# A first linear map in seven block products, and running sums kept in PSUM

## The chip, the cores and the metric

The kernel runs on one core of a Trainium2 chip. A core has a matrix engine (TensorE, PE in the profile), a vector engine (VectorE, DVE), a scalar engine (ScalarE, ACT), a general engine (GpSimd, POOL) and SyncE (SP), which here only issues transfers (DMA). Each works through its own instructions in order and waits on semaphores for the others. SBUF is the working memory of 128 partitions; PSUM, eight banks of 512 floats per partition, is where TensorE puts its results and can add to what is there. The metric is the device time of one execution in microseconds (us): the median of the timed runs.

## The reference

Two layers on x of shape (B, N, C) = (16, 1024, 256), all in float32. Each layer computes h = relu(layernorm(x)) and adds its result to x.

```
# layer 0, per batch: a graph product, then attention with 4 heads
Wg   = adj * A_s(channel means of h)
g    = relu(einsum('bcn,bnm->bcm', h^T, Wg) * para);  q from g
k, v = h @ kv_w
x    = x + softmax(q k^T * scale) v
# layer 1
A_hat = (A + I) * dinv[:, None] * dinv[None, :]
agg   = einsum('nm,bmd->bnd', A_hat, h)
z     = relu(batchnorm(agg @ W1.T + b1))      # 512 features
out   = batchnorm(z @ W2.T + b2)              # 256 features
x     = x + out
```

The batch normalizations take mean and variance over all 16 x 1024 rows. So everything up to the first map (agg @ W1.T + b1) is done for all batches, and only then does the second map start.

## The kernel before

**Stages.** The first stage runs over the 16 batches. For batch b its order on TensorE is: attention of b (`attention`, L351: four steps of eight score tiles and eight value products), the graph product of b+1 with its k, q and v (`graph`, L291), and then the two parts of layer 1 for batch b: the A_hat stage and the first map (`linear1`, L533, and `linear1_out`, L616). The second stage reads the results of the first map (z1) back from memory, normalizes them and does the second map, in pairs of column blocks. At the end (L1128 to L1170) the output is scaled by the second batch normalization, turned by TensorE, added to x1 (the output of layer 0, read back from memory) and stored.

**Order.** Nothing is reordered by a scheduler: each engine's instructions stand in the order in which the code issues them. Work of other batches is placed by hand. `graph` has a list `between` of steps to run ahead of its block c (L796 to L815), `linear1` has three hooks (`between[0]` to `between[2]`, L591 to L614). `more(c)` makes f_w, the weighted adjacency of block c of the next batch (two passes on ScalarE, one on VectorE, L262 to L266); `turn_h` transposes h of the next batch, 32 x 32 blocks on VectorE (L278) and 32 small DMAs issued by POOL (L285). `prepare_start` and `prepare_end` normalize the input of batch b+2 (statistics on VectorE, the inverse root on POOL, eight passes on ScalarE); `prepare_row` sends the channel sums to memory and back as a row (L248, L249); `again` loads x once more.

**A_hat stage.** agg is a product of 2 x 2 blocks done with seven block products instead of eight. The sums and differences of h are made on VectorE (L544 to L547); those of A_hat (`thirds`) are made once and loaded per batch. Each product fills a PSUM bank of its own with four matmul calls, and VectorE adds the banks up (L593 to L613).

**First map.** For each half g of the columns (512 nodes) and each of the four blocks of 128 features, two calls over the two halves of the 256 channels: 16 calls per batch. ScalarE adds the bias while it copies to SBUF (L637), for the last two blocks of a batch VectorE (L635). VectorE then takes batch statistics (L641), and SP stores z (L642). Batch 15 has an order of its own (`very_last`). Batch 14's first-layer work comes after the attention of batch 15, directly ahead of that of batch 15; its third hook (L845) holds the last part of batch 15's attention, its normalization and the turning of W2.

**Buffers.** `ps_s` has three PSUM buffers of two banks (score tiles, products, map results); a new tile takes the buffer that was given up first. `pp` has eight SBUF buffers of 4 KB per partition (score exponentials, `thirds`, turned h) and two more for accumulators; `w4` has five (f_w, para, agg, z).

**End.** `AHEAD` (L25) is the number of batches of x1 that are loaded ahead (`load_x1`, L871, 1 MB each, in buffers of 8 KB that the second stage also uses). z2, the output of the second map, holds the nodes in their order; x1 is loaded with eight consecutive nodes per partition. So `scaled` (L1134) reads z2 in steps of eight elements into a second tile, and TensorE turns that one:

```
src = src.rearrange("p (q i) -> p i q", i=NC)[:, i0:i1, :]
```

Of the kernel before, what the change touches and what calls it, by code (L numbers as in the profile page):

```python
# [17 lines left out]
P = 128  # L18
# [5 lines left out]
I32 = mybir.dt.int32  # L24
AHEAD = 7  # L25
LIMIT = 1e18
# [3 lines left out]
def fast_path(  # L30
# [34 lines left out]
    x1_d = [dram.tile([N, C], F32, tag=f"fx1_{b}", name=f"fx1_{b}") for b in range(B)]  # L65
    row_d = [dram.tile([N], F32, tag=f"frow_{b}", name=f"frow_{b}") for b in range(B)]
    t_d = [dram.tile([P, 4, 512], F32, tag=f"ft_{k}", name=f"ft_{k}") for k in range(3)]
    z1_d = [dram.tile([P, FC, 512], F32, tag=f"fz1_{t}", name=f"fz1_{t}") for t in range(TT)]
# [86 lines left out]
    with ExitStack() as stage:  # L155
# [377 lines left out]
        def linear1(b, h1, thirds, between):  # L533
# [14 lines left out]

            def product(ps, left, right):
                for m in range(KH):  # L550
                    nc.tensor.matmul(  # L551
                        ps,
                        left[:, m, :],
                        right(m),
                        start=(m == 0),
                        stop=(m == KH - 1),
                    )

# [27 lines left out]
            ]  # L586
            m1 = new(1)
            product(m1, a(0, 0), resident(0, 0))
            u1 = kept(1)
            nc.scalar.copy(u1, m1)  # L590
            m2 = new(2)  # L591
            product(m2, a(0, 1), resident(1, 0))
            nc.vector.tensor_add(agg[0][:, 0, :], u1, m2)  # L593
            m6 = new(6)
            product(m6, s2, third(0))
            u2 = kept(2)
            nc.vector.tensor_add(u2, u1, m6)
            between[0]()
            m7 = new(7)
            product(m7, s3, third(1))  # L600
            u3 = kept(3)
            nc.vector.tensor_add(u3, u2, m7)
            between[1]()
            m5 = new(5)
            product(m5, s1, resident(0, 1))
            nc.vector.tensor_add(agg[1][:, 1, :], u3, m5)
            nc.vector.tensor_add(u2, u2, m5)
            m4 = new(4)
            product(m4, a(1, 1), third(2))
            nc.vector.tensor_sub(agg[0][:, 1, :], u3, m4)  # L610
            m3 = new(3)
            product(m3, s4, resident(1, 1))
            nc.vector.tensor_add(agg[1][:, 0, :], u2, m3)  # L613
            between[2](agg)  # L614

        def linear1_out(b, g, aggT, parts=range(0, FC, 2)):  # L616
            t = NH * b + g
            for f2 in parts:
                ps = ps_s.tile([P, 2, 512], F32, tag="s", name=f"f_zps_{t}_{f2}")
                z = w4.tile([P, 2, 512], F32, tag="w4", name=f"f_z1_{t}_{f2}")  # L620
                for i in range(2):
                    f = f2 + i
                    for d in range(CC):
                        nc.tensor.matmul(  # L624
                            ps[:, i, :],
                            w1T[:, d, ts(f, P)],
                            aggT[:, d, :],
                            start=(d == 0),
                            stop=(d == CC - 1),
                        )  # L630
                for i in range(2):
                    f = f2 + i
                    if g + 1 == NH and f2 + 2 == FC and b + 1 < B:

                        nc.vector.tensor_scalar_add(z[:, i, :], ps[:, i, :], b1_t[:, f : f + 1])  # L635
                    else:
                        nc.scalar.activation(  # L637
                            z[:, i, :], ps[:, i, :], AF.Identity, bias=b1_t[:, f : f + 1]
                        )
                for i in range(2):  # L640
                    nc.vector.bn_stats(st1[:, f2 + i, t, :], z[:, i, :])  # L641
                nc.sync.dma_start(z1_d[t][:, f2 : f2 + 2, :], z)  # L642

        def linear1_all(b, h1, thirds, early, late, last):


            def second(agg):
                linear1_out(b, 0, agg[0])
                last()
                linear1_out(b, 1, agg[1])  # L650

            def very_last(agg):

# [12 lines left out]

            linear1(b, h1, thirds, [early, late, second if b + 1 < B else very_last])

# [10 lines left out]


        ahatT = big.tile([P, NC, N], F32, tag="ahatT", name="f_ahatT")
        deg = small.tile([P, NC], F32, tag="deg", name="f_deg", bufs=1)
        rsum = small.tile([P, NC], F32, tag="rsum", name="f_rsum", bufs=1)
# [4 lines left out]
        def turn_adj(i, copy):  # L688
            ps = ps_s.tile([P, NC, P], F32, tag="s", name=f"f_adjps_{i}")
            for m in range(NC):  # L690
                nc.tensor.transpose(ps[:, m, :], adj_t[i][:, ts(m, P)], ident)
            copy(ahatT[:, :, ts(i, P)], ps)

# [13 lines left out]
        def diagonal():  # L707
            on = unused("d").rearrange("p (m q) -> p m q", q=P)
            for m in range(NC):
                block = ahatT[:, m, ts(m, P)]  # L710
                nc.gpsimd.tensor_mul(on[:, m, :], block, ident)
                nc.gpsimd.tensor_add(block, block, ident)
            nc.vector.tensor_reduce(diag, on, AX.X, ALU.add)
# [6 lines left out]
        def roots_row():  # L720
            t = pp.tile([P, N], F32, tag="p", name="f_drow")
            ps = ps_s.tile([P, NC, P], F32, tag="s", name="f_drowps")
            for c in range(NC):
                nc.tensor.transpose(ps[:, c, :], dinv[:, c : c + 1].to_broadcast([P, P]), ident)
            nc.scalar.copy(t, ps.rearrange("p c q -> p (c q)"))
            drow.append(t)
# [14 lines left out]
        with tc.manual_schedule(engines={ENG.PE, ENG.Activation, ENG.DVE, ENG.Pool, ENG.SP}):  # L741
# [17 lines left out]
            def turn_w1():  # L759
# [9 lines left out]
                    4: [lambda: weights(0, 6), lambda: prepare_end(1), lambda: again(0)],  # L769
                    5: [lambda: weights(0, 7)],  # L770
                    7: [lambda m=m: row_sums(m) for m in range(4)],
# [5 lines left out]
            for b in range(B):  # L777
# [14 lines left out]
                def more(c):  # L792
# [4 lines left out]
                    0: [  # L797
                        more(2), lambda: turn_h(b + 1), left[0], left[1], left[2], more(3),
                        left[3], left[4], more(4),
# [65 lines left out]
    with ExitStack() as stage:  # L865
        big = stage.enter_context(tc.tile_pool(name="fbig2", bufs=1))
        io = stage.enter_context(tc.tile_pool(name="fio", bufs=AHEAD))

        xts = {}

        def load_x1(b):  # L871

            xts[b] = io.tile([P, NC, C], F32, tag="x1", name=f"f_x1t_{b}")
            nc.sync.dma_start(xts[b], x1_d[b].rearrange("(p i) d -> p i d", i=NC))

        st2 = big.tile([P, CC, TT, 6], F32, tag="st2", name="f_st2")
        with tc.manual_schedule(engines={ENG.PE, ENG.Activation, ENG.DVE, ENG.Pool, ENG.SP}):
# [39 lines left out]
            class Pair:  # L917
# [5 lines left out]
                def load(self):  # L923
                    p = self.p
                    t0, t1 = self.t

                    def two(name):
                        t = io.tile([P, 2, 2, 512], F32, tag="x1", name=f"f_z{name}_{p}")
                        return t[:, 0], t[:, 1]

                    self.t2, self.t3 = two("t23")
                    one, other = two("b1")
                    self.b[0, 0] = fetch(t0, 0, one)
                    self.b[1, 0] = fetch(t0, 2)
                    self.b[0, 1] = fetch(t1, 0, other)
                    one, self.t4 = two("b2")
                    self.b[1, 1] = fetch(t1, 2, one)

# [86 lines left out]
            def fetch_all(t):  # L1025
                z = io.tile([P, FC, 512], F32, tag="x1", name=f"f_zz_{t}")
                nc.sync.dma_start(z, z1_d[t])
                for f2 in range(0, FC, 2):
                    zs[t, f2] = z[:, f2 : f2 + 2, :]

# [24 lines left out]
            for p in SEVEN:  # L1055
# [20 lines left out]
                else:  # L1076
                    for t in rest:
                        fetch_all(t)
                    for t in range(TT - 2, TT):
                        for f2 in range(0, FC, 2):  # L1080
                            zs[t, f2] = fetch(t, f2)
                    for n in range(AHEAD):
                        load_x1(n)
# [40 lines left out]


            turned_z = {}

            def finish(b, c, i0, i1):  # L1128
                if i0 == 0:
                    turned_z[b, c] = lasting.tile(  # L1130
                        [P, NC, P], F32, tag="z", name=f"f_zo_{b}_{c}", bufs=4
                    )

                def scaled(out, src):  # L1134
                    src = src.rearrange("p (q i) -> p i q", i=NC)[:, i0:i1, :]
                    s, t = bn2.s[:, c : c + 1], bn2.t[:, c : c + 1]
                    if c == 0:
# [4 lines left out]
                if b + 1 < B:  # L1142
                    scaled(turned_z[b, c][:, i0:i1, :], z2[:, c, b, :])
                else:
                    for g in range(NH):
                        scaled(turned_z[b, c][:, i0:i1, ts(g, P // NH)], last[g, c])

            for b in range(B):
# [3 lines left out]
                for i0 in range(0, NC, 4):  # L1152
                    ps = ps_out.tile([P, 4, C], F32, tag="out", name=f"f_outps_{b}_{i0}")
                    for c in range(CC):
                        if b == 0:
                            finish(b, c, i0, i0 + 4)
                        for i in range(4):
                            nc.tensor.transpose(
                                ps[:, i, ts(c, P)], turned_z[b, c][:, i0 + i, :], ident
                            )  # L1160
# [4 lines left out]
                for i0, ps in zip(range(0, NC, 4), outs):  # L1165
                    here = xt[:, i0 : i0 + 4, :]
                    nc.vector.tensor_add(here, here, ps)
# [517 lines left out]
```

## Time and profile before

| what | us |
|---|---|
| median of three runs | 2504.25 (2500.96 to 2507.36) |
| the profiled execution | 2502.86 |
| its span | 2501.1 |
| mean granted clock of TensorE | 0.992 of full speed |

The span runs from the first to the last instruction of the profiled execution; the 1.8 us around it are the launch. The costliest groups on TensorE, by line (a matmul call of float32 is recorded as two instructions; "busy" counts overlapped instructions once):

| line | what | records | busy, us |
|---|---|---|---|
| L362 | attention scores | 2048 | 458.1 |
| L403 | attention values | 2048 | 453.6 |
| L308 | graph product | 1024 | 444.7 |
| L551 | A_hat stage (four groups) | 896 | 398.0 |
| L326, L341 | k, q and v | 768 | 227.7 |
| L624 | first map | 512 | 222.5 |

A row of the profile's groups gives line, engine and operation, then output and inputs with their shapes, the number of instructions, their busy time and mean duration in ns, and last the idle time of the engine just before them with what ended it. A row of a timeline gives start, length, engine, line, operation and, in brackets, the idle time before it and its releaser. The chain of waits follows the work that ended last back through its releasers.

### The profile page before, as it was taken

How to read it: one execution, taken by the hardware profiler on the slowest of the kernel's cores; microseconds unless marked ns; L12 is line 12 of the kernel's file. 1: busy time of each engine (PE TensorE's matmuls, PEld its weight loads, DVE VectorE, ACT ScalarE, POOL GpSimd, SP SyncE). 2: the span in 40 equal slices, each digit the busy share in tenths (PEclk: the TensorE clock that was granted, in tenths of full speed). 3: DMA queues.
4: the chain of work that ended last, by engine and by line, in shares of the span. 5: the costliest groups of instructions: out<-in, count | busy, mean ns of one | idle time of the engine just before them, and what ended most of it. 6: DMA issues, size and time to landing. Idle time of an engine off the chain costs nothing.

```text
span 2501.1 us, 24402 instructions
## 1 busy us (share of the span) xinstructions
PE 2432.2 (97%) x8122; PEld 1074.5 (43%) x8122; DVE 1625.7 (65%) x2223; ACT 1302.0 (52%) x1854; POOL 328.1 (13%) x577
## 2 busy tenths in 40 slices
PE   7999999999999999999999999999999999999984
PEld 4443444434343434344443434343444434444443
DVE  4786667484838475665848393857667586567665
ACT  7845545454636464554536363645555456256543
POOL 2030202020110302020202002030202020000012
PEclk9999999999999999999999999999999999999997
DMA  5031414131322324141322232242424120445549
GB/s 168 7 129 59 135 59 135 59 104 53 107 84 63 115 62 132 59 135 59 118 70 87 71 94 91 59 127 59 135 60 135 59 68 29 148 172 180 212 159 355
DMA packets 169239, 263.42 MB, mean 105 GB/s; under 512 B 37009, under 2 KB 120465, under 8 KB 166545
## 3 DMA queue, kind: packets, MB, share of 16 engines
q1 hardware_dynamic: 148944, 229.23, 28.4%
q0 software_dynamic: 20160, 32.55, 4.1%
q8 instruction: 66, 1.08, 0.2%
q14 instruction: 69, 0.56, 0.1%
HBM read 157.82 MB, written 70.31 MB: 91 GB/s over the span
## 4 chain that ended last, share of the span: by engine, by line
PE 82%; DMA 7%; DVE 5%; ACT 3%; issue 1%; SPq 1%; POOL 1%; DVEq 0%; POOLq 0%; ACTq 0%
PE f_s L362 15%; PE f_o L403 15%; PE f_aps L551 15%; PE f_gps L308 13%; PE f_zps L624 8%; PE f_vps L341 4%; PE f_kps L326 4%; PE f_zx L953 3%; PE f_zm L953 2%; DMA out_dram<-f_x1t 2%; PE f_z2ps L889 2%; DVE f_acc L379 1%; DMA f_hT<-f_hQ 1%; SPq L467 1%; DMA frow<-f_sums 1%
## 5 line engine op out<-in xcount | busy, mean ns | idle before, releaser
L370 ACT ACTIVATE f_p<-f_s 128x1024 f32<-128x1024 f32 x512 | 477.3, 1046 | 145.4 <-PE f_s L362 144.0
L379 DVE TENSOR_TENSOR f_acc<-f_acc,f_p 128x1024 f32<-128x1024 f32 x384 | 470.5, 1225 | 41.1 <-DVE f_acc L379 1.4
L362 PE MATMUL f_s<-f_qT,f_kT 64*128 64x512 f32 x2048 | 458.1, 596 | 0.0
L403 PE MATMUL f_o<-f_p,f_v 128*64 128x512 f32 x2048 | 453.6, 595 | 0.0
L308 PE MATMUL f_gps<-f_w,f_h_a 128*128 128x512 f32 x1024 | 444.7, 594 | 2.2 <-DVE f_w L266 2.2
L285 POOL DMA_DIRECT2D f_hT<-f_hQ x480 | 235.7, 499 | 1226.0 <-DVE f_hQ L278 838.3
L362 PEld LDWEIGHTS f_s<-f_qT,f_kT 64*128 64x128 f32 x2048 | 189.4, 185 | 265.9 <-ACT f_p L370 121.6
L308 PEld LDWEIGHTS f_gps<-f_w,f_h_a 128*128 128x128 f32 x1024 | 192.8, 190 | 250.4 <-issue 229.3
L403 PEld LDWEIGHTS f_o<-f_p,f_v 128*64 128x64 f32 x2048 | 141.4, 137 | 304.3 <-issue 274.0
L624 PE MATMUL f_zps<-f_aggT,f_w1T 128*128 128x512 f32 x512 | 222.5, 592 | 0.0
L266 DVE SCALAR_TENSOR_TENSOR f_w<-f_w,f_adj 128x1024 f32<-128x1024 f32 x128 | 155.1, 1213 | 83.2 <-ACT f_w L265 76.2
L262 ACT ACTIVATE f_w<-f_row,f_col 128x1024 f32<-128x1024 f32 x128 | 148.2, 1158 | 52.3 <-DMA f_row<-frow 47.7
L637 ACT ACTIVATE f_z<-f_zps,f_b 128x512 f32<-128x512 f32 x98 | 62.1, 684 | 202.9 <-PE f_zps L624 202.9
L219 ACT ACTIVATE f_h_a<-f_x,f_shift_a,f_rstd_a 128x256 f32<-128x256 f32 x128 | 75.0, 587 | 175.5 <-DVE f_shift_a L214 175.5
L641 DVE BATCH_NORM_STATS2 f_st<-f_z 128x6 f32<-128x512 f32 x128 | 82.2, 684 | 124.6 <-ACT f_z L637 124.6
L219 ACT ACTIVATE f_h_b<-f_x,f_shift_b,f_rstd_b 128x256 f32<-128x256 f32 x128 | 64.6, 587 | 170.7 <-DVE f_shift_b L214 170.7
L624 PEld LDWEIGHTS f_zps<-f_aggT,f_w1T 128*128 128x128 f32 x512 | 97.2, 190 | 122.0 <-issue 122.0
L265 ACT ACTIVATE f_w<-f_w 128x1024 f32<-128x1024 f32 x128 | 135.3, 1057 | 4.1
L593 DVE TENSOR_TENSOR f_aggT<-f_u,f_aps 128x512 f32<-128x512 f32 x16 | 11.0, 688 | 180.5 <-PE f_aps L551 180.5
L326 PE MATMUL f_kps<-f_hT,f_kvw 128*128 128x512 f32 x256 | 114.6, 595 | 6.4 <-DMA f_hT<-f_hQ 5.5
L551 PE MATMUL f_aps<-f_ahatT,f_hs 128*128 128x512 f32 x256 | 115.1, 592 | 0.0
L551 PE MATMUL f_aps<-f_ahatT,f_h_b 128*128 128x512 f32 x256 | 112.9, 593 | 0.9 <-ACT f_z L637 0.9
(151 smaller groups left out, 2453.5 us busy)
## 6 DMA issues: line engine op xcount, KB each, us to landing
f_t<-ft SPq DMA_DIRECT2D x84, 512.0 KB, 8.2
f_x<-in_x_dram SPq DMA_DIRECT2D x32, 1024.0 KB, 6.0
fz<-f_z SPq DMA_DIRECT2D x64, 512.0 KB, 3.5
f_zb<-fz SPq DMA_DIRECT2D x36, 512.0 KB, 4.5
f_para<-in_L_gnn_para_dram SPq DMA_DIRECT2D x32, 512.0 KB, 4.7
f_att<-f_oT SPq DMA_DIRECT2D x512, 32.0 KB, 1.9
fx<-f_x SPq DMA_DIRECT2D x16, 1024.0 KB, 6.0
f_x1t<-fx SPq DMA_DIRECT2D x16, 1024.0 KB, 8.2
```

The source lines that it names most:

```text
L219: nc.scalar.activation(self.h[:, c, :], self.xt[:, c, :], AF.Relu, bias=self.shift[:, c : c + 1], scale=self.rstd[:, c : c + 1], accum_out ...
L262: nc.scalar.activation(w, rows[b], AF.Abs, bias=cols[b][:, c : c + 1], scale=0.5 / C)
L266: nc.vector.scalar_tensor_tensor(w, w, 1.0, adj_t[c], ALU.subtract, ALU.mult)
L285: queue.dma_start(to[ts(k, 32), ts(a, 32 * NC)], t[ts(a, 32), k].rearrange("i c r -> i (c r)"),)
L308: nc.tensor.matmul(gps[d][:, ts(g, 512)], hs[b][:, c, ts(d, P)], w[:, ts(g, 512)], start=(c == 0), stop=(c == NC - 1),)
L326: nc.tensor.matmul(ps[:, ts(g, 512)], kvw_t[:, e, ts(d, P)], hT[e][:, ts(g, 512)], start=(e == 0), stop=(e == CC - 1),)
L362: nc.tensor.matmul(ps[:, e, :], kT[rows_e, pair, ts(m, P)], qT[rows_e, pair, ts(g, 512)], start=True, stop=True,)
L370: nc.scalar.activation(p, ps, AF.Exp)
L379: nc.vector.tensor_add(acc_of[s], acc_of[s], p)
L403: nc.tensor.matmul(o_of[s][e * HD : (e + 1) * HD, :], v[:, m, ts(2 * pair + e, HD)], p[:, e, :], start=(m == 0), stop=(m == NC - 1),)
L551: nc.tensor.matmul(ps, left[:, m, :], right(m), start=(m == 0), stop=(m == KH - 1),)
L624: nc.tensor.matmul(ps[:, i, :], w1T[:, d, ts(f, P)], aggT[:, d, :], start=(d == 0), stop=(d == CC - 1),)
```

## The change

- **First map.** Batches 0 to 14 use `linear1_seven` in place of `linear1_out`: the product of 2 x 2 blocks (feature halves by channel halves by node halves) with seven block products of two calls each, 14 in place of 16. Sums of W1 are made once (`make_w1_sums`, in the first graph stage), stored, and loaded for every batch on SP in the first hook (512 KB). Sums of agg are made on VectorE, partly in place. A running sum is kept in PSUM: one product after the other is added to it, and ScalarE copies it out between (with the bias twice, once without). The third hook is called in the middle of the map.
- **A_hat stage.** The products 1, 6, 5 and 3 go into one bank as a running sum, which ScalarE copies out after each; VectorE does four additions where it did six.
- **Nodes in the order of the end.** The columns of A_hat are permuted when A is turned (`columns`), with the diagonal and the scaling row, so that z2 comes out in the order in which the end wants it: `scaled` works in place on contiguous data, and the second tile goes.
- **Loads ahead.** `AHEAD` is 9: x1 is loaded in halves of 512 KB; batches 0 to 6 as before into the buffers of the second stage (now 14 of 4 KB), 7 and 8 into the four z buffers after the last products. Pairs and the last tiles use 4 KB tiles.
- **Order.** `turn_h` goes ahead of `more(2)` in the graph stage. In `linear1_out`, now used by batch 15 alone, the bias is always ScalarE's.

The diff, cut to its core:

```diff
-            def product(ps, left, right):
+            def product(ps, left, right, more=False):
...
-                        start=(m == 0),
+                        start=not more and m == 0,
...
-            m1 = new(1)
-            product(m1, a(0, 0), resident(0, 0))
-            u1 = kept(1)
-            nc.scalar.copy(u1, m1)
...
+            ps, sum_ps = new(2), new(1)
+            product(sum_ps, a(0, 0), resident(0, 0))
+            u1, u2, u3 = kept(1), kept(2), kept(3)
+            nc.scalar.copy(u1, sum_ps)
+            product(ps, a(0, 1), resident(1, 0))
+            nc.vector.tensor_add(agg[0][:, 0, :], u1, ps)
+            product(sum_ps, s2, third(0), True)
+            nc.scalar.copy(u2, sum_ps)
             between[0]()
             m7 = new(7)
             product(m7, s3, third(1))
+            nc.vector.tensor_add(u2, u2, m7)
             between[1]()
+            product(sum_ps, s1, resident(0, 1), True)
+            nc.scalar.copy(u3, sum_ps)
+            nc.vector.tensor_add(agg[1][:, 1, :], u3, m7)
             m4 = new(4)
             product(m4, a(1, 1), third(2))
+            nc.vector.tensor_sub(agg[0][:, 1, :], u2, m4)
+            product(sum_ps, s4, resident(1, 1), True)
+            nc.scalar.copy(agg[1][:, 0, :], sum_ps)
+            between[2](agg, spare[:, 0:2] if b + 2 == B else None)
...
+        def linear1_seven(b, agg, sums, up, middle):
...
+            nc.vector.tensor_sub(t3, part(1, 1), part(0, 1))
+            nc.vector.tensor_sub(part(0, 1), part(0, 1), part(0, 0))
+            t1 = part(0, 1)
+            nc.vector.tensor_sub(t2, part(1, 1), t1)
+            nc.vector.tensor_sub(t4, part(1, 0), t2)
...
+            m2, sum_ps = new(2), new(1)
+            mult(both(sum_ps), w1_part(0, 0), part(0, 0))
+            biased(0, 0, sum_ps)
+            mult(both(m2), w1_part(0, 1), part(1, 0))
+            nc.vector.tensor_add(c[0, 0], c[0, 0], m2)
+            store(0, 0)
+            stats(0, 0)
+            m7 = new(7)
+            mult(both(m7), sums[:, 2], t3)
+            mult(both(sum_ps), sums[:, 1], t2, True)
+            biased(1, 0, sum_ps)
+            middle()
+            m4 = new(4)
+            mult(both(m4), w1_part(1, 1), t4)
+            nc.vector.tensor_add(c[1, 0], c[1, 0], m7)
+            nc.vector.tensor_add(c[1, 0], c[1, 0], m4)
+            store(1, 0)
+            mult(both(sum_ps), sums[:, 0], t1, True)
+            nc.scalar.copy(up, sum_ps)
+            stats(1, 0)
+            add_biased(1, 1, both(m7))
+            store(1, 1)
...
+            mult(m3, sums[:, 3], part(1, 1))
+            add_biased(0, 1, m3)
+            store(0, 1)
+            stats(1, 1)
+            stats(0, 1)
...
-            copy(ahatT[:, :, ts(i, P)], ps)
+            copy(columns(i), ps.rearrange("p m (q i) -> p m i q", i=NC))
...
-                    5: [lambda: weights(0, 7)],
+                    5: [lambda: weights(0, 7), make_w1_sums],
...
-                        more(2), lambda: turn_h(b + 1), left[0], left[1], left[2], more(3),
+                        lambda: turn_h(b + 1), more(2), left[0], left[1], left[2], more(3),
...
+            for b in range(AHEAD - 2, AHEAD):
+                load_x1(b, lasting, "z", 4)
...
-                    scaled(turned_z[b, c][:, i0:i1, :], z2[:, c, b, :])
+                    ready[b, c] = z2[:, c, b, :]
+                    at = ready[b, c][:, i0 * P : i1 * P]
+                    scaled(at, at)
```

In `linear1_seven`, `biased` is ScalarE's copy with the bias (two of 128 x 512), `add_biased` VectorE's sum of a product, the bias and `up` (two of 128 x 512), `stats` two batch statistics, `store` one DMA of 512 KB.

## The prediction

> **What bounds the kernel now.** I began with the page's busy times and its chain of waits.
>
> ```profile
> PE 2432.2 (97%) x8122; PEld 1074.5 (43%) x8122; DVE 1625.7 (65%) x2223; ACT 1302.0 (52%) x1854; POOL 328.1 (13%) x577
> PE 82%; DMA 7%; DVE 5%; ACT 3%; issue 1%; SPq 1%; POOL 1%; DVEq 0%; POOLq 0%; ACTq 0%
> L624 PE MATMUL f_zps<-f_aggT,f_w1T 128*128 128x512 f32 x512 | 222.5, 592 | 0.0
> ```
>
> TensorE is the path. The last line is the map to be changed: 222.5 us, no idle time before it. Each matmul call is recorded as two instructions (512 records for 256 calls), so a call costs 222.5/256 = 0.87 us; 592 ns is one pipelined record, not the rate. Then the chain in order of time around batch 1:
>
> ```profile
> 442.40 24.03 PE f_aps L551 x56
> 466.43 13.73 PE f_zps L624 x32
> 480.16 7.07 PE f_s L362 x32
> ```
>
> A_hat stage, map and attention follow one another on TensorE without a gap: 13.73 us is 16 calls at 0.858. A call taken away here is time taken away, if nothing else becomes late. VectorE's timeline shows who might:
>
> ```profile
> 481.53 1.28 DVE L641 BATCH_NORM_STATS2 f_st<-f_z 128x6 f32<-128x512 f32 x2
> 483.24 1.23 DVE L376 TENSOR_TENSOR f_acc<-f_p,f_p 128x1024 f32<-128x1024 f32 x1 [0.44 <-ACT f_p L370]
> 484.57 7.88 DVE L379 TENSOR_TENSOR f_acc<-f_acc,f_p 128x1024 f32<-128x1024 f32 x6
> 494.13 1.23 DVE L266 SCALAR_TENSOR_TENSOR f_w<-f_w,f_adj 128x1024 f32<-128x1024 f32 x1 [1.68 <-ACT f_w L265]
> ...
> 538.32 1.18 DVE L266 SCALAR_TENSOR_TENSOR f_w<-f_w,f_adj 128x1024 f32<-128x1024 f32 x1
> 539.42 2.36 DVE L278 STREAM_TRANSPOSE f_hQ<-f_h_a 128x1024 f32<-128x1024 f32 x2
> ```
>
> In attention (480.1 to 536.4) VectorE idles only 0.44 and 1.68 us; from 494 on it works without a pause, and it reaches the next graph stage (TensorE there at 536.43) about 2 us late. Last, the windows of the end (columns: PE, PEld, DVE, ACT, POOL busy, clock, DMA share, GB/s):
>
> ```profile
> 2405.00:2425.00 20.00, 15.55 (x50) 8.44 (x50) 11.71 (x24) 6.91 (x4) 1.74 (x4) 0.91 0.04 18
> 2425.00:2450.00 25.00, 17.34 (x123) 14.45 (x122) 24.56 (x22) 16.04 (x8) 11.15 (x15) 0.94 0.94 329
> 2450.00:2475.00 25.00, 13.18 (x87) 11.12 (x86) 19.86 (x19) 12.60 (x7) 6.45 (x11) 0.88 1.02 405
> 2475.00:2501.00 26.00, 6.21 (x29) 5.44 (x27) 6.04 (x6) 0.00 (x0) 3.19 (x6) 0.57 0.77 308
> ```
>
> The last 76 us are bound by the DMA engines (0.94 and 1.02 busy), after 20 us in which these idle.
>
> **The map in seven products.** 14 calls instead of 16 in batches 0 to 14 (batch 15 keeps the plain form): 2 x 0.858 = 1.72 us off TensorE per batch. Is it ever made to wait? I laid the three engines out by hand with durations of before, for one batch, t = 0 at the start of the A_hat stage (442.23).
>
> A_hat stage: seven products of 3.43 us as before. The running sum now stays in one bank, so the product after each copy waits for ScalarE. Copies 1 and 2 (0.59 us, row L590) are 3 us early. The third stands on ScalarE behind the eight normalizations of the next input (4.78 us from 458.80 on). These begin earlier now, since their statistics no longer wait behind L597: their gate is the VectorE addition of product 7 (ends 14.6), so they run 14.9 to 19.6, the copy ends at 20.2, and TensorE wants it at 20.6: **0.3 us to spare**.
>
> Map: TensorE from 24.03. VectorE makes four sums (0.69 each, row L544) from 24.85, when ScalarE's last copy is out, to 27.6; product 7 wants the first at 27.46 (there at 25.5). The biased copies take ScalarE 1.27 (row L637, two): 25.95 to 27.2, wanted 29.18; 31.1 to 32.4, wanted 32.61: **0.2 to spare**. TensorE ends at 36.05 instead of 37.77. VectorE has more: 2.8 (sums), 3 x 1.22, 4 x 0.7, 8 statistics at 0.65, together 14.5 us where it had 8 x 0.65 + 1.41 = 6.6. With its waits it ends at 41.6, 5.6 us after TensorE (before: 482.8, 2.7 after). In the changed program's list of waits the first three score tiles wait for VectorE, ScalarE, VectorE: I read these as the banks of product 4 (free at 34.9), the running sum (35.5) and product 7 (37.6, after the biased addition), wanted at 36.05, 36.9, 37.8: **0.2 to spare**, no stall.
>
> Cover for VectorE's lateness: 2.9 us relative to TensorE, less the 2.1 idle above (the row's round trip through memory, which ended the 1.68, is asked for 3.5 us sooner), leaves 0.7 to 0.8. Attention absorbs it: the output bank is freed 3.5 us ahead of need now (497.68 against 501.25). In the graph stage `turn_h` goes ahead of `more(2)`: VectorE does 2.3 us of transposes first, so f_w of block 2 is ready at 6.0 us after TensorE's start, wanted at 6.9 (two blocks of 3.46). Behind it, block 3 is ready at 9.6, wanted 10.3. Cost nothing; without cover 1 us per us of lateness, 14 times.
>
> Batch 14 is different: its hook (last attention part, statistics, w2 transposes, eight normalizations) now sits in the middle of the map, ahead of ScalarE's copy of the sum, whose bank batch 15 needs. The chain add, statistics, POOL, normalizations, which began at 2165.17, begins near 2162; batch 15 starts near 2173.0, its end moves from 2197.6 to 2197.0. Gain 0.6, not 1.7. Sum: 14 x 1.72 + 0.6 = **-24.7 us**. Three waits with 0.2 to 0.3 to spare: I charge +1 (between 0 and 15 x 0.7 = 10).
>
> The z blocks use the same five buffers in turn; the next f_w that needs one comes a whole attention step after its store. Loading the four weight sums (512 KB per batch) is hidden: issued on SP before the A_hat stage, wanted 27 us later, f_t of that size lands in 8.2. Behind it on SP stands nothing before the first z store at 28.9.
>
> `turn_h` earlier: TensorE waits for f_hT seven times, 5.5 us in all, 0.3 to 1.6 each. POOL's 32 issues start 1.1 earlier, less the 0.7 lateness: 0.4 x 7, near -3; between -5.5 and +5 (each of 14 later by 0.4). Since each batch of eight issues waits for landings, not for VectorE, I take **-1**.
>
> **Start.** `make_w1_sums` puts a store on SP ahead of the para loads. Row L303: para is issued at 51.27, and TensorE waits for it (0.99 at 59.31). The store waits for VectorE: f_w of block 7 ends 51.1, four additions of 256 at 0.42 (row L912) end 52.8, so para leaves 2.1 later: **+2** (0 to +3.5 with the store in its way). The permuted copies of A read PSUM with a stride; L1138 does so from PSUM at 0.772 for 512 against 0.684 (L637): +0.2 to 0.4 for each of eight, absorbed before para.
>
> **End.** Two more f_x1t loads go into the z buffers as these come free (2413 and 2416), in the idle window. From 2424 on there are 16 stores and 7 loads (of 1.05 MB each) instead of 16 and 9: 2.1 MB less at 350 GB/s (26.4 MB in the 76 us of the last three windows) is -6. The finishing pass reads in order: ScalarE's 2.26 us becomes about 1.05 (row of exponentials, 1024 wide), VectorE's at most stays 1.24; the pitch of 3.41 per batch was VectorE's and doesn't bind. First store up to 1 us sooner, not counted. Here a rule speaks against the change: the Trainium skill, "DMA: Bandwidth & Descriptors", section Bandwidth, wants transfers of at least 1 MiB, with 6.15 us for 1 MB and 0.95 for 64 KB; between these I estimate 3.4 for 512 KB, so 0.6 lost per MB on the halved loads, 7 x 0.6 = 4, and the end would gain 2. The row: stores of 512 KB were already two thirds of the traffic at 405 GB/s, above the rule's 341. With many in flight the size doesn't show; I take **-6** (-2 to -8).
>
> Sum: -24.7 + 1 - 1 + 2 - 6 = -28.7. The profiled execution took 2502.86 (span 2501.1): 2474.2. The median of the runs shown, 2504.25, is 1.4 above it, so **2475**.
>
> **Rivals.** (a) The small margins fail: ScalarE and VectorE come half a us later than laid out, and TensorE waits at three places, 0.7 per batch, +10: 2485 to 2487. For: margins of 0.2. Against: the starts come from this trace, with the wake-up after each wait in them. 18%. (b) More comes: f_hT waits vanish (-4) and the end gives 8: 2468. 14%. (c) Slower: VectorE is late at the graph stage. Margin 0.9 us at block 2; each further us costs 14. The gain is gone at 2.0 beyond the margin, and 0.3% slower at 2.6, that is a lateness 3.4 us greater than mine; at 4 it is 2518. For: VectorE is saturated from 494 to 542, and the map's VectorE work more than doubles. Against: most of the 7.9 us more lies under the map itself, which left VectorE idle 2 to 3.5 us between its groups. 6%. (d) Both the end and the margins disappoint, and the lateness costs half: within 0.3%, 4%.
>
> **Numbers.** Forecast 58% (own range 2468 to 2481). What a measurement can tell from no change is 0.3%, 7.5 us. Faster: forecast, (a), (b): 0.90; same 0.04; slower 0.06. Range 2464 to 2489: (a) and (b) inside.
>
> **What would show it.** Map groups on TensorE: 28 records per batch, 12.0 us between A_hat stage and first scores, with no idle time before them; the score tiles of step 0 without a wait for VectorE; L266 not ending TensorE's idle time in the graph stage; para about 2 us later; DMA busy at 2385 to 2400 of the new time, and the last 70 us at 350 GB/s. Wrong would be idle time before the third bank reuse of A_hat, the fourth of the map, or a DMA end that still takes 76 us.

## The result, and the profile after

| | before | after |
|---|---|---|
| median of four runs, us | 2502.71 (2500.96 to 2507.36) | 2464.26 (2463.73 to 2464.29) |
| span of the profiled execution, us | 2501.1 | 2461.9 |

The ratio is 0.985, with a 95% interval of 0.9836 to 0.9865: 38.5 us less, where 28.7 were forecast. The time lies inside the range, a quarter of a us above its lower end. It lies outside the forecast's own 2468 to 2481, below it, where rival (b) had put its 2468.

The busy times of the page, to compare with those of before:

```profile
PE 2399.5 (97%) x8062; PEld 1058.3 (43%) x8062; DVE 1700.3 (69%) x2314; ACT 1308.5 (53%) x1887; POOL 325.8 (13%) x577
```

TensorE has 60 records less (15 batches, 2 calls of 2 records each) and is busy 32.7 us less; it is still the path. Then TensorE's timeline of the same batch as before (start, length, engine, line, operation, tiles, shapes, count; the idle time before a row would stand at its end in brackets):

```profile
458.84 3.60 PE L552 MATMUL f_aps<-f_ahatT,f_hs 128*128 128x512 f32 x8
462.27 3.60 PE L647 MATMUL f_zps<-f_aggT,f_w1T 128*128 128x512 f32 x8
465.70 3.60 PE L647 MATMUL f_zps<-f_zt,f_w1s 128*128 128x512 f32 x8
469.14 1.88 PE L647 MATMUL f_zps<-f_zt,f_w1T 128*128 128x512 f32 x4
470.85 1.88 PE L647 MATMUL f_zps<-f_aggT,f_w1s 128*128 128x512 f32 x4
472.57 1.02 PE L647 MATMUL f_zps3a<-f_aggT,f_w1s 128*128 128x512 f32 x2
473.43 1.02 PE L647 MATMUL f_zps3b<-f_aggT,f_w1s 128*128 128x512 f32 x2
474.38 7.14 PE L363 MATMUL f_s<-f_qT,f_kT 64*128 64x512 f32 x32
```

The map is 28 records, and from its first to the first score it takes 474.38 - 462.27 = 12.11 us, where it took 13.83. No row has a bracket: none of the three thin margins failed. VectorE's timeline of the same attention and of the start of the graph stage (TensorE enters that at 530.72):

```profile
475.73 0.74 DVE L677 SCALAR_TENSOR_TENSOR f_z<-f_zps3a,f_b,f_u 128x512 f32<-128x512 f32 x1
476.39 0.74 DVE L677 SCALAR_TENSOR_TENSOR f_z<-f_zps3b,f_b,f_u 128x512 f32<-128x512 f32 x1
477.05 2.46 DVE L686 BATCH_NORM_STATS2 f_st<-f_z 128x6 f32<-128x512 f32 x4
479.43 1.21 DVE L377 TENSOR_TENSOR f_acc<-f_p,f_p 128x1024 f32<-128x1024 f32 x1
...
522.14 7.87 DVE L380 TENSOR_TENSOR f_acc<-f_acc,f_p 128x1024 f32<-128x1024 f32 x6 [0.47 <-DVE f_acc L377]
...
533.09 2.33 DVE L279 STREAM_TRANSPOSE f_hQ<-f_h_a 128x1024 f32<-128x1024 f32 x2
535.35 1.18 DVE L267 SCALAR_TENSOR_TENSOR f_w<-f_w,f_adj 128x1024 f32<-128x1024 f32 x1
```

VectorE ends the map's work at 479.5, 5.1 us after TensorE (forecast: 5.6), and has one pause of 0.47 us in the whole attention. It reaches the transposes 2.4 us after TensorE's start; f_w of block 2 is ready at 536.5, 5.8 after it, 1.1 before it is wanted.

Where the 39.2 us of the span went, by the starts of the stages on TensorE:

| stage | before | after | difference | forecast |
|---|---|---|---|---|
| start to the first A_hat stage | 169.3 | 170.4 | +1.1 | +2 |
| map, batches 0 to 14 | 208.4 | 184.2 | -24.2 | -24.7 + 1, with the row of A_hat |
| k, q, v, without the first | 214.0 | 207.6 | -6.4 | -1 |
| attention | 902.8 | 901.6 | -1.3 | 0 |
| A_hat | 387.1 | 386.4 | -0.7 | in the row of the map |
| second stage to the first store | 226.8 | 227.1 | +0.3 | 0 |
| first store to the end | 76.9 | 68.7 | -8.2 | -6 |

Inside the row of the second stage lie 1.1 us that are lost up to its last products, and 0.7 that are gained behind them. The windows of the end, first after and then before (columns: PE, PEld, DVE, ACT, POOL busy, clock, DMA share, GB/s):

```profile
2361.00:2386.00 25.00, 24.17 (x57) 10.51 (x56) 9.55 (x18) 3.30 (x4) 0.55 (x1) 1.00 0.37 120
2386.00:2393.00 7.00, 3.60 (x18) 3.12 (x17) 5.54 (x12) 7.00 (x7) 0.56 (x1) 0.73 0.51 173
2393.00:2410.00 17.00, 13.32 (x92) 11.17 (x92) 16.76 (x17) 8.40 (x9) 6.27 (x12) 0.91 0.91 322
2410.00:2462.00 52.00, 19.82 (x150) 15.81 (x148) 29.52 (x30) 0.00 (x0) 11.10 (x21) 0.79 0.89 361
```

```profile
2416.00:2424.00 8.00, 3.55 (x20) 2.65 (x19) 6.72 (x13) 3.54 (x2) 0.55 (x1) 0.83 0.00 0
2424.00:2501.00 77.00, 37.72 (x240) 32.00 (x238) 51.47 (x46) 29.04 (x15) 21.43 (x32) 0.79 0.89 342
```

The 7 us ahead of the first store, in which the DMA engines had stood idle (0.00 in the 8 us from 2416 before), now carry 173 GB/s. From the first store on, 69 us at 322 and 361 GB/s are 24.2 MB; before, 77 us at 342 were 26.3.

The largest gap between forecast and result is in k, q and v. The rows of k on the two pages (busy time and mean ns, then the idle time before, with what ended most of it), before and after:

```profile
L326 PE MATMUL f_kps<-f_hT,f_kvw 128*128 128x512 f32 x256 | 114.6, 595 | 6.4 <-DMA f_hT<-f_hQ 5.5
```

```profile
L327 PE MATMUL f_kps<-f_hT,f_kvw 128*128 128x512 f32 x256 | 113.5, 593 | 1.0 <-DVE f_qT L336 0.8
```

The waits for h (f_hT), 5.5 us in 7 places before, are gone. The change touches these stages only by its order (`turn_h` ahead of `more(2)`), so that was the first suspect.

### The profile page after: what moved, and what is told of

Read it like the earlier page. It is cut to its first block, busy times and chain, and to the rows that moved or that the text cites. A ratio compares the mean times of both kernels' runs of the same rounds, so it can differ in the third digit from the quotient of the medians.

```text
span 2461.9 us, 24485 instructions
## 1 busy us (share of the span) xinstructions
PE 2399.5 (97%) x8062; PEld 1058.3 (43%) x8062; DVE 1700.3 (69%) x2314; ACT 1308.5 (53%) x1887; POOL 325.8 (13%) x577
## 4 chain that ended last, share of the span: by engine, by line
## 5 line engine op out<-in xcount | busy, mean ns | idle before, releaser
L552 PE MATMUL f_aps<-f_t,f_hs 128*128 128x512 f32 x256 | 112.6, 592 | 1.6 <-DVE f_hs L546 1.6
L342 PE MATMUL f_vps<-f_kvw,f_hT 128*128 128x256 f32 x512 | 113.1, 379 | 0.0
L342 PEld LDWEIGHTS f_vps<-f_kvw,f_hT 128*128 128x128 f32 x512 | 97.3, 190 | 20.1 <-issue 6.0
L377 DVE TENSOR_TENSOR f_acc<-f_p,f_p 128x1024 f32<-128x1024 f32 x64 | 76.3, 1192 | 29.9 <-ACT f_p L371 29.9
```

What stands on the lines that cost most here:

```text
L342: nc.tensor.matmul(ps[:, i, :], hT[e][:, ts(c4 + i, P)], kvw_t[:, e, C : 2 * C], start=(e == 0), stop=(e == CC - 1),)
L552: nc.tensor.matmul(ps, left[:, m, :], right(m), start=not more and m == 0, stop=(m == KH - 1), skip_group_check=more,)
```

## The experiments

All times are medians; the changed kernel's is 2464.26, measured with the result and not again. The experiments ran in three sets, and the kernel before took 2500.88 beside e1 to e4, 2498.25 beside e5 to e8 and 2501.75 beside e9 to e12. So a difference of 1 to 3 us from the changed kernel, or between sets, is not settled by the times alone; there the stages of the profiles, one for each kernel, have to speak. For k, q and v the number followed is the excess: what the last 15 of these stages take over 15 times the shortest of them (13.77). It is 7.4 us before and 1.0 after.

### Is it the order?

Back, in the changed kernel, and alone, in the kernel before:

```diff
-                        lambda: turn_h(b + 1), more(2), left[0], left[1], left[2], more(3),
+                        more(2), lambda: turn_h(b + 1), left[0], left[1], left[2], more(3),
```

> Theory (the order did it): the changed kernel with f_w of block 2 ahead of the transposes of h again. The transposes start 1.1 us later against TensorE than in the changed kernel and 0.5 later than before the change, so the waits for f_hT come back, 5.5 us of before and up to 0.5 more in each of 15 batches: 2470 to 2477. Rival (the waits went because the transfers of h land sooner, 2.4 us where it was 3.1, as other transfers have moved away): waits for f_hT stay below 1 us, 2463.5 to 2465.5.

> Theory (the order did it): the kernel before with the transposes of h ahead of f_w of block 2, nothing else. The issues start 1.1 us sooner, most of the 5.5 us of f_hT waits go, block 2 is still in time: 4 to 6 us less than before, 2496.5 to 2498.5. Rival (other transfers that moved): no change, 2502 to 2503.

Measured: 2465.1 (2463.3 to 2466.0) and 2502.59 (2500.2 to 2505.2), beside 2500.88 for the kernel before. By the times it was the rival in both: the order is worth about 1 us in the changed kernel and nothing in the other. In the profiles the excess is 2.7 (e1) and 11.9 (e2): the order is worth 1.7 there in the changed kernel, and without the rest of the change, asking for h sooner even made more waits. The transfers of h land in 4.0 us (median) in e2, where it was 3.1 before: the first of them is issued 1.6 us sooner after the start of the stage (3.7 instead of 5.4, means of 14 stages), into DMA engines that the six loads of the A_hat sums (f_t, 3.1 MB, issued as the graph stage begins) keep busy.

### The map alone

> The changed kernel with the sixteen-call map of before in batches 0 to 14, and without sums of W1, their store and loads. Theory (the map is worth what its calls are, and its VectorE work costs nothing later): 14 x 1.72 + 0.2 more, 1.1 less at the start: 23 more, 2487 to 2488. Rival (its VectorE work is paid for later, in attention and the graph stage): less than 22 more. Rival (it also brings something later, f_hT waits gone because the row is asked for sooner): 26 to 30 more.

```diff
-                linear1_seven(b, agg, sums[0], up, last)
+                linear1_out(b, 0, agg[0])
+                last()
+                linear1_out(b, 1, agg[1])
```

Measured: 2491.55 (2488.9 to 2497.0), 27.3 more: the rival that the map brings something besides its calls, though the reason it gave (the row is asked for sooner) is not what the next runs show. TensorE's waits in e3 show what:

```profile
PE f_kps L327 <- DMA f_hT<-f_hQ: 7.2, 6, 1.9
```

The row gives the sum, the number and the longest wait. The waits for h are back (an excess of 10.8 us), though the order is the changed kernel's; the map itself is 24.2 longer. The profile is of the slowest run (2496.95), so most runs have less of these waits. And the runs are further apart again, 8 us, where the changed kernel's lie within 1.

### What of the map takes the waits away?

Besides its calls the map has one load per batch on SP, and it takes two buffers of the pool `pp` (the sums of W1, and two sums of agg). That pool of eight is given out in turn. Before, a batch takes 40 buffers, so that every batch begins at the same one; now 42. In e5 the map is plain, but the sums of W1 are loaded; in e6 nothing is loaded, and two buffers are taken for nothing:

```diff
+                    for n in range(2):
+                        t = pp.tile([P, N], F32, tag="p", name=f"f_gap{n}_{b}")
+                        nc.gpsimd.memset(t[:, 0:1], 0.0)
```

> The changed kernel with the sixteen-call map of before in batches 0 to 14, as in e3, but the sums of W1 are still made, stored and loaded for every batch (and then not used). It asks why the f_hT waits came back in e3 (10.8 us over the plain stages, where the changed kernel has 1.0). Theory (the one more transfer per batch on SP shifts the turns of the transfers): the waits are below 3 us again and the time is 2481 to 2486. Rival (it is the map's own timing): the waits stay at 7 to 12 us, 2489 to 2495.

> As e3, with two unused buffers taken from the pool of the score exponentials in every batch (one element of each set to zero by GpSimd) and no load: the pool turns as in the changed kernel, SP's transfers as before. Theory (it is the turn of the buffers, so which buffers h and the sums of A_hat land in): f_hT waits below 3 us, 2481 to 2486. Rival (it is the transfers or the map's timing): 7 to 12 us of waits, 2489 to 2495.

Measured: 2488.16 (e5) and 2485.81 (e6, 2485.0 to 2486.4). In both profiles the excess of k, q and v is 0.1. The two unused buffers alone, with no other transfer and the plain map, take the waits away. e5 took one buffer and a load, so it fits either theory, and its time missed the expectation by 2: its profile reaches the first A_hat stage 2.3 us later than that of e6, having the store of the sums at the start. What the turn moves is seen in the view of a tile, in its last line, issue to landing in us, least, median and most. First the loads of the A_hat sums (f_t) and then the transfers of h (f_hQ) in e3:

```profile
DMA to landing us min/median/max: 2.6/9.3/14.2
```

```profile
DMA to landing us min/median/max: 1.6/3.9/8.8
```

and the same two in e6:

```profile
DMA to landing us min/median/max: 2.6/6.4/10.6
```

```profile
DMA to landing us min/median/max: 1.6/2.3/6.7
```

The loads are as many and of the same size, and are issued at the same place, within 0.4 us on the mean; with the turn of e6 they land in two thirds of the time, and the transfers of h behind them too. Then the same two things were done to the kernel before, and in e10 the loads were moved out of the way:

> The kernel before with two unused buffers taken in every batch from the pool of the score exponentials (one element of each set to zero by GpSimd), nothing else: what e6 did to the plain map in the changed kernel. Theory (the turn of that pool makes the f_hT waits): most of the 7.4 us that k, q and v take over their shortest stage go, 5 to 7 us less than before, with a smaller spread: 2491 to 2496. Rival (it needs the order of the changed kernel too): within 1.5 of before, 2497 to 2502.

> The kernel before with the six loads of the A_hat sums (3.1 MB) not ahead of the graph stage but at its end, behind the load of x. Theory (the transfers of h are slow because they share the DMA engines with these loads): h lands in 1.7 to 2.5 us instead of 3.1, the waits for f_hT go, 5 to 7 us less than before, 2491 to 2496; the loads still land before the third product of the A_hat stage, some 13 us after they are issued. Rival (something else makes them slow): within 1.5 of before. Rival (the loads come late instead): slower than before.

```diff
-                    if 0 < b < B - 2:
-                        thirds = load_thirds(b)
                     qkv = graph(b + 1, between)
...
+                    between[8].append(lambda: late_thirds.append(load_thirds(b)))
```

Measured: 2495.98 (e9) and 2494.64 (e10), beside 2501.75 for the kernel before: 5.8 and 7.1 less. The excess is 2.7 and 0.1. In e10, with 3.1 MB out of the way, the view of h's transfers shows

```profile
DMA to landing us min/median/max: 1.6/1.7/5.6
```

By itself e10 leaves a rival: h now takes its buffers ahead of the sums, so the turn has moved too. The kernel before settles it. Its last graph stage (from 2034) has no loads of the A_hat sums and the old turn, and h lands there in 1.7 us (1.6 to 3.6). The DMA engines are 0.22 busy in the first 15 us of that stage, 0.81 in the one from 1218, and 0.24 in a stage of e10. All four combinations of order and turn are on record (the runs differ in map and end besides), with the medians to landing in us:

| order of `turn_h` | turn of the pool | run | loads (f_t) | h (f_hQ) | excess |
|---|---|---|---|---|---|
| as before | as before | before | 7.7 | 3.1 | 7.4 |
| changed | as before | e2, e3 | 9.1, 9.3 | 4.0, 3.9 | 11.9, 10.8 |
| as before | changed | e9, e1 | 6.6, 7.4 | 2.2, 2.3 | 2.7, 2.7 |
| changed | changed | e6, after | 6.4, 7.3 | 2.3, 2.4 | 0.1, 1.0 |

So the waits are shown to come with these loads, which keep the DMA engines busy while h is sent, and the turn of the pool is shown to be enough to make that worse or better. Asking sooner adds waits with the old turn and takes off about two us with the new one. Why the loads land faster with one turn than with the other stays open. It isn't one place in SBUF: in e6 every batch is fast, whichever buffers its turn gives it.

### The A_hat stage

> The changed kernel with the A_hat stage of before (a bank for every product, six additions on VectorE instead of four additions and four copies on ScalarE). Theory (the running sum there is worth only the end of batch 15's stage, 0.65): 2464 to 2466. Rival (VectorE's two more additions, 1.4 us per batch, come late at the graph stage, where about 1.0 was to spare): 0.4 x 14 = 6 more, 2469 to 2472. Rival (the small margin of the third copy behind the eight normalizations costs something in the changed kernel): faster than 2463.

The diff is the change of the A_hat stage, taken back. Measured: 2464.17. The running sum is worth nothing measurable there: without it batch 15's stage is 25.2 instead of 25.8 (shorter, where the theory had it 0.65 longer), batch 14's map 14.8 instead of 14.6. VectorE's two more additions stand in a stage in which it has pauses, and cost nothing.

### What VectorE's lateness costs

```diff
             stats(1, 1)
             stats(0, 1)
+            for n in range(4):
+                nc.vector.tensor_add(t_spare, c[0, 1][:, 0, :], c[0, 1][:, 1, :])
```

> The changed kernel with four more additions of 512 on VectorE at the end of the map of batches 0 to 14, 2.9 us per batch, whose results nobody reads. VectorE's only pause until the graph stage is 0.5, f_w of block 2 is ready there about 1.0 before TensorE wants it. Theory (the price of lateness): 2.9 - 0.5 - 1.0 = 1.4 late in 14 batches, 20 more, 2481 to 2488. Rival (attention or the order behind it absorbs it): 2464 to 2467. Rival (it is late at f_hT as well and at the score exponentials' buffers): 2492 and more.

Measured: 2497.55 (2493.9 to 2500.6), 33 more, in the region of the last rival. But the place is another than all three had. TensorE's list of waits has a new first row, and none for f_w in the graph stages of batches 2 to 15 (two waits for f_hT, 1.9 us, are back):

```profile
PE f_s L363 <- ACT f_p L371: 19.6, 14, 1.7
```

These are scores that wait for ScalarE, in the last step of attention. ScalarE's timeline there, in the changed kernel:

```profile
516.04 1.02 ACT L446 COPY f_recs<-f_rec 32x32 f32<-32x32 f32 x4 [3.87 <-DVE f_rec L438]
517.87 7.44 ACT L371 ACTIVATE f_p<-f_s 128x1024 f32<-128x1024 f32 x8 [0.81 <-PE f_s L363]
```

and in e8, where TensorE begins the step 5.5 us later:

```profile
524.26 1.02 ACT L446 COPY f_recs<-f_rec 32x32 f32<-32x32 f32 x4 [6.56 <-DVE f_rec L438]
525.31 7.44 ACT L371 ACTIVATE f_p<-f_s 128x1024 f32<-128x1024 f32 x8
```

ScalarE has the copies of the reciprocals ahead of the exponentials of the last step, and the reciprocals are VectorE's. In the changed kernel the exponentials still wait 0.81 us for TensorE: that is the margin. In e8 the copies stand 2.8 us later in the stage (44.4 after its start instead of 41.7), and TensorE waits for ScalarE. 14 attention stages take 1.95 us or more longer (58.29 instead of 56.34), 27.9 in all; so 0.8 of the 2.8 was covered, the 0.81 of the row, and the rest was paid for in full in each stage. The graph stage begins late with everything else and finds its f_w ready. The span of this profile is 36.2 longer (its run took 2500.01); the rest of that is batch 15's A_hat stage (30.0 instead of 25.8), 1.7 each in k, q, v and at the start, and less than 1 elsewhere.

### The end

> The changed kernel without the two loads of x1 into the z buffers; the halves and the reading in order stay. Theory: these two loads are 6 of the 9 us gained at the end (2.1 MB at 350 GB/s), the rest is the shorter pitch of VectorE: 2469.5 to 2471.5. Rival (the loads are all): 2473 and more. Rival (the pitch is all, the loads are hidden anyway): 2464 to 2466.

Measured: 2469.52, 5.3 more. From the first store to the end its profile takes 74.9, where the changed kernel has 68.7 and the kernel before 76.9. So the two loads are 6.2 of the end, as forecast. The 2.0 that are left would come from what e4 keeps (reading in order, and loads in halves), but this size is not shown: in e2, e9 and e10, which leave the end of the kernel before as it is, it takes 75.5 to 75.7, so what e4 keeps is worth 0.6 to 2.0. Profiles with the end of the changed kernel lie between 68.0 and 69.3. The first store comes 0.7 sooner behind the last products.

> The changed kernel with x1 loaded in pieces of 256 KB instead of 512 KB. Theory (with many transfers in flight the size doesn't show): 2463 to 2466. Rival (the skill's figures, 6.15 us for 1 MB and 0.95 for 64 KB: by a line between these, in my estimate, 256 KB takes 2.0, so 1.2 more per MB than with 512 KB, for the seven loads in the stretch that the DMA engines bound): 8 more, 2471 to 2474.

```diff
-                nc.sync.dma_start(t, x1_d[b].rearrange("(p h i) d -> p h i d", h=NH, p=P)[:, h])
+                half = x1_d[b].rearrange("(p h i) d -> p h i d", h=NH, p=P)[:, h]
+                for i in range(0, NC // NH, 2):
+                    nc.sync.dma_start(t[:, i : i + 2], half[:, i : i + 2])
```

Measured: 2466.07 (2465.6 to 2469.1), 1.8 more, just outside my theory and a quarter of what I had estimated from the Trainium skill's figures ("DMA: Bandwidth & Descriptors", section Bandwidth). In its profile, of the slowest run (2469.11), the end takes 71.5, 2.8 more. Smaller pieces do cost something here with many in flight, but far less than a line between the page's figures would say: the stretch behind the first stores still moves 412 GB/s, where it was 417 (25 us from 2410 in both).

### A faster version

> The changed kernel with two moves: the sums of W1 are made and stored behind the loads of para of the first batch (step 7 instead of 5), and the six loads of the A_hat sums stand at the end of the graph stage, as in e10. Theory: the start gains 1.6 (the five profiles with the store ahead of para reach the first A_hat stage at 170.4 to 172.1, those without it at 169.1 to 169.5), and the 1.0 of f_hT waits that are left goes: 2461 to 2463. Rival (the loads of the A_hat sums come late for the third product): 2466 and more.

```diff
-                    5: [lambda: weights(0, 7), make_w1_sums],
-                    7: [lambda m=m: row_sums(m) for m in range(4)],
+                    5: [lambda: weights(0, 7)],
+                    7: [make_w1_sums] + [lambda m=m: row_sums(m) for m in range(4)],
```

and the edit of e10. Measured: 2462.11 (2460.9 to 2463.4), ratio to before 0.984 (0.9824 to 0.9856). It is 2.2 under the changed kernel, and all its runs lie under that kernel's. But the two intervals overlap, and the changed kernel did not run beside it, so by the times the gain is not shown. For it speak the stages: TensorE's wait for q behind para (0.8 in the changed kernel) is gone, the excess of k, q and v is 0.1 instead of 1.0, and h lands in 1.7 us. The first A_hat stage begins at 169.4 instead of 170.4; but so it does in e1, with the store ahead of para, which the five profiles of the expectation leave out.

## Why the prediction was right, and where it was not

- **The map, -24.7:** right. 14 x 1.72 = 24.1 were measured, and for batches 14 and 15 together 0.8, where 0.6 were forecast: 0.2 in batch 14's map and 0.6 in batch 15's A_hat stage. It was laid out the other way round (the map longer, the A_hat stage free of waits); in the run ScalarE's turning of W2 stands in front of the bank that is wanted in the map (1.4 us of wait), and the A_hat stage still waits 1.6 for VectorE's sums of h.
- **Three thin margins, +1:** they held; nothing was lost there.
- **f_hT, -1 (-5.5 to +5):** this is the mis-sized term: 6.4. The step that failed is the one that looked at the issues alone, "POOL's 32 issues start 1.1 earlier, less the 0.7 lateness". The difference, 0.4, was too small: the first issue comes 1.4 earlier in the stage (4.0 instead of 5.4 on the mean). But that is worth 1 to 2 us in the changed kernel (e1) and nothing without it (e2). What I took as given was how long the transfers take to land. The two buffers that the map takes out of `pp` changed that, from 3.1 to 2.4 us: with the old turn they land in 3.1 to 4.0 whatever the order, with the new one in 2.2 to 2.4 (e1, e2, e3, e6, e9). The prediction followed that pool only to the reuse of its buffers, not to the transfers that land in them.
- **The start, +2:** 1.1 in this profile. Para leaves 3.1 us later (54.41), not 2.1, and lands in 5.1 where it took 7.0, so TensorE goes on 1.2 later (60.48). L1138 was misread as the price of a stride in PSUM: the same pass in order, L1254, takes 0.762 where it took 0.772. The profiles with the store ahead of para reach the first A_hat stage at 169.4 to 172.1, those without at 169.1 to 170.7, so a single profile doesn't settle the size.
- **The end, -6:** the loads gave that (6.2). Reading in order, which I had said doesn't bind, and the loads in halves are worth 0.6 to 2.0 more. The earlier first store, which I had not counted, is 0.7. VectorE's pitch per batch fell from 3.41 to 2.98 us. The rule on transfer sizes, taken at nothing, cost little in e11, with pieces of half the size; halves against whole loads were not tried.
- **VectorE's lateness, cost nothing; rival (c):** it cost nothing, and the price beyond the margin was right in the one run that went beyond it (14 per us, margin 0.8). The place was wrong: the margin ends at ScalarE's copies in the last step of attention, with 0.81 to spare, not at block 2 of the graph stage, where 1.1 is to spare.
- **Not foreseen:** 1.3 less in attention (three stages of before were 0.3 to 0.6 longer than the others), 1.1 more up to the last products of the second stage. The last shows in waits for VectorE (f_zm, 1.1 before, 2.0 after); neither was tried.
- **Rival (b)**, waits for h gone and an end of 8, was what came, with 6.4 and 8.2 where it had 4 and 8. It had 14%, and for the waits it named no reason; that they went is luck as far as the prediction is concerned.

## What to carry to other kernels

A step that takes or gives back buffers of a shared pool moves every later tenant of it, the targets of transfers too. Before a gain is put down to arithmetic, take the buffers without the work: here about 6 us of 38 came from that. And where a wait for a small transfer varies from run to run, look for the large ones that are issued just ahead of it; moving those took the waits off here, asking sooner did not. The cost of a late engine is found by following what stands behind its results in the other engines' queues, not only where its next output is wanted.

## What was not expected of the hardware

- The same six loads of 512 KB, issued within 0.4 us of the same moment of the stage, land in 9.3 us (median) or in 6.4, according to which buffers of a pool their neighbours hold (e3, e6). It was measured, not explained.
- The spread of the kernel before goes with the waits for h: beside e10 its 19 runs lie between 2497.4 and 2508.1, the 6 of e10, with no such wait in its profile, between 2493.3 and 2496.0, and the 4 of the changed kernel within 1 us.
- The transfers of h, 32 KB each, landed in 1.7 us (median) with the six loads out of the way, and in 4.0 with these 3.1 MB under way (e10, e2).
